# Self-attention's row products regrouped: five groups of four matmuls a step, and seven PSUM banks handed out as one set

## The chip, the cores and the metric

The kernel runs on one NeuronCore of a Trainium2 chip. Its time is the device time of one execution in microseconds (us). The kernel before took 2029.76 us (median of 3 runs, 2025.14 to 2033.86).

## The reference

Two transformer blocks act on `x` of shape (4, 1024, 256): cross attention over 64 context rows, then a self-attention block with a mixture of experts, then a second cross attention and a second mixture of experts. The change lies in the self-attention, of which this is the core (16 heads of width 16, 1024 rows a batch):

```python
scores = jnp.einsum('bhqd,bhkd->bhqk', q, k) / np.float32(np.sqrt(hd))
scale = jax.nn.sigmoid(jnp.einsum('bhsd,hd->bhs', q, scale_w)) * 2.0
scores = scores * scale[..., None]
aw = jax.nn.softmax(scores, axis=-1)
out = jnp.einsum('bhqk,bhkd->bhqd', aw, v).transpose(0, 2, 1, 3).reshape(b, s, d)
```

A softmax takes the row's maximum off before the exponential, and the kernel computes that maximum exactly.

## The kernel before

**Units and steps.** Self-attention is cut into 32 units: a batch, half of its queries (512), and four heads (L658, class `Unit`). Each unit takes eight steps in each of two passes.

- The first pass (`first`, L677) multiplies queries by keys so that a query is a PSUM partition, and VectorE takes the maximum of 512 keys at a time (L694). A step makes four such products, one for each head.
- The second pass (`second`, L712) runs LEAD = 11 steps behind. It multiplies the other way round, so that a key is a partition, adds the negated maxima with a product of ones (`ones_r`, `self.m`), and ScalarE takes the exponential out of PSUM (L726). A step makes four of these too.
- `weigh` (L728) multiplies the exponentials of the step before by the values and adds the result up in the bank `acc`.

Queries and keys are kept as a leading and a remaining half side by side, so that a product of one head has a contraction of 32 rows. Each first product is two matmuls (parts f0 and f1 below), each second product three (s0, s1 and s2, the one with ones). All are 512 columns wide. Head j of a unit sits on partitions 32j to 32j+31, so that the matmuls of the four heads use different rows of the PE array and can run side by side. I call such a set of up to four a group, heads 0 and 1 the low heads and heads 2 and 3 the high heads.

**The order of a step.** It is written out by hand in the loop at the end of `self_attention` (L623); TensorE and VectorE keep the program's order (`in_order`). `round_` (L953) is called twice, with `weigh` between the calls:

| group | before, from row groups of low heads | from row groups of high heads |
|---|---|---|
| 1 | s0 | f0 |
| 2 | s1 | f1 |
| 3 | s2 | none |
| | weigh (four column groups) | |
| 4 | f0 | s0 |
| 5 | f1 | s1 |
| 6 | none | s2 |

After group 6 come the fillers: small pieces of other work which `on(step)` doles out by a credit of 1.5 a step, among them the transposes and products that bring a later tile in (`enter`), turn the maxima (`maxima`, L697) or the accumulated result (`done`, L740), and finish a tile (`leave`). A filler takes one PSUM bank, which ScalarE or VectorE reads out. In the order of each engine the read of a filler follows the exponentials and the maxima of its step.

**PSUM.** Of eight banks one is `acc`. Three rotate for first products (pool `first`), four rotate for second products and fillers (pool `bank`). A new tile in a bank waits until the last reader of the bank's former tile is done. In the eleven steps before the second pass starts, the first products take every other tile from `bank`.

Of the kernel before, what the change touches and what calls it, by code (L numbers as in the profile page):

```python
# [26 lines left out]
ALU = mybir.AluOpType  # L27
AX = mybir.AxisListType
# [3 lines left out]
P = 128  # L32
# [36 lines left out]
def two_blocks(  # L69
# [19 lines left out]
    nc = tc.nc  # L89
# [3 lines left out]
    banks = {}  # L93

    @contextmanager
    def psum(stage, **bufs):

        with ExitStack() as stack:
            for tag, n in bufs.items():
                pool = tc.tile_pool(name=f"{stage}_{tag}", bufs=n, space=PSUM, reuse_waits="tile")  # L100
                banks[tag] = stack.enter_context(pool)
            yield

    def new(pool, shape, tag, dt=F32, bufs=None):
        return pool.tile(shape, dt, tag=tag, name=tag, bufs=bufs)

    def two_banks():
        return new(banks["two_banks"], [P, 1024], "two_banks")

    def bank():  # L110
        return new(banks["bank"], [P, 512], "bank")

    def side():
        return bank()[:, :256]
# [4 lines left out]
    def placed(engine, ins):  # L119
        return tc.keep_in_program_order(ins) if engine in in_order else ins  # L120

    def matmul(*args, **kw):
        return placed(nc.tensor, nc.tensor.matmul(*args, **kw))  # L123
# [7 lines left out]
    def on_dve(ins):  # L131
        return placed(nc.vector, ins)
# [64 lines left out]
    def on_all(pool, first, n, queue, width=D):  # L197

        at = ROWS.index(first) * D
        t = new(pool, [P, n, width], f"row_{first}")  # L200
        queue.dma_start(
            out=t.rearrange("p n d -> p (n d)"), in_=rows[at : at + n * width].partition_broadcast(P)
        )
        return [t[:, i] for i in range(n)]
# [304 lines left out]
    class Entrance:  # L509


        def __init__(self, even, pool):
            self.pool = pool
            self.k_rows = [new(even, [P, 4, S], "k_rows0", F32R)]
            self.vals_1 = [new(even, [P, TB * H * K1 + ROW], "vals_10")]
            self.wq4 = new(pool, [P, 2, D], "wq4")

            self.wz = new(pool, [P, 2, P], "wz")
            self.gb_half = new(pool, [P, 2], "gb_half")
            at = ROWS.index("gb") * D  # L520
            nc.scalar.dma_start(out=self.gb_half, in_=rows[at : at + D].rearrange("(m p) -> p m", p=P))
            self.n1g, self.n1b = on_all(pool, "n1g", 2, nc.scalar)
            (self.moe_gb,) = on_all(pool, "last", 1, nc.scalar, E)
# [99 lines left out]
    def self_attention(ent, first_batch):  # L623
# [3 lines left out]


        with tc.tile_pool(name="sa1", bufs=1) as one, tc.tile_pool(name="sa2", bufs=2) as work:
            acc = new(banks["acc"], [P, 512], "acc")  # L630
            gb_half, n1g, n1b, moe_gb = ent.gb_half, ent.n1g, ent.n1b, ent.moe_gb
            ent.k_rows.append(new(one, [P, 4, S], "k_rows1", F32R))
            ent.vals_1.append(new(one, [P, TB * H * K1 + ROW], "vals_11"))
# [24 lines left out]
            class Unit:  # L658
# [15 lines left out]
                    self.part = new(small, [P, 4, 4, 2], "tops", bufs=3)  # L674
                    yield 0

                def first(self, s, js, half, alone):  # L677

                    assert self.b["entered"] == TB
                    i, at = s // 2, s % 2  # L680
                    for j in js:
                        if half == 0:
                            self.ps[j] = bank() if alone and j % 2 else new(banks["first"], [P, 512], "first")
                        r = slice(j * ROW, (j + 1) * ROW)
                        matmul(
                            self.ps[j],
                            self.q[r, half, i * P : (i + 1) * P],
                            self.b["k"][r, self.g, at * 512 : (at + 1) * 512],
                            start=half == 0,
                            stop=half == 1,  # L690
                        )
                        if half:
                            on_dve(
                                nc.vector.tensor_reduce(self.part[:, i, j, at : at + 1], self.ps[j], AX.X, ALU.max)  # L694
                            )

                def maxima(self):  # L697
                    top = new(small, [P, 4, 4], "top4", bufs=2)
# [13 lines left out]
                def second(self, k, js, part):  # L712

                    if part == 0 and js[0] == 0:
                        self.es.append(new(work, [P, 4, 512], "e"))
                    for j in js:
                        if part == 0:
                            self.ps[j, 2] = bank()
                        ps = self.ps[j, 2]
                        r = slice(j * ROW, (j + 1) * ROW)  # L720
                        if part < 2:
                            keys = self.b["k"][r, self.g, k * P : (k + 1) * P]
                            matmul(ps, keys, self.q[r, part], start=part == 0, stop=False)
                        else:
                            matmul(ps, ones_r[r], self.m[r], start=False, stop=True)
                            nc.scalar.activation(self.es[k][:, j], ps, AF.Exp)  # L726

                def weigh(self, k):  # L728

                    for j in range(4):  # L730
                        v = (k * H + 4 * self.g + j) * K1
                        matmul(
                            acc[j * ROW : (j + 1) * ROW],
                            self.b["v_flat"][:, v : v + ROW],
                            self.es[k][:, j],
                            start=k == 0,
                            stop=k == TB - 1,
                        )
# [74 lines left out]

            first = new(one, [P, E], "first")
            nc.vector.tensor_scalar(first, iota_e, float(E), None, ALU.subtract)
            nc.vector.tensor_copy(next_row, region)
            low = new(one, [P, 4, E], "low")
# [130 lines left out]
            for step in range(-6, 8 * NU + 80):  # L948
                n1, n2 = step // 8, (step - LEAD) // 8
                k2 = (step - LEAD) % 8  # L950
                u1, u2 = units.get(n1) if step >= 0 else None, units.get(n2) if step >= LEAD else None

                def round_(js, others):  # L953
                    for part in range(3):
                        if u2:
                            u2.second(k2, js, part)
                        if u1 and part < 2:
                            u1.first(step % 8, others, part, False)

                if u1 and not u2:  # L960
                    for part in range(2):
                        u1.first(step % 8, range(4), part, True)
                else:
                    round_((0, 1), (2, 3))
                before_ = step - LEAD - 1
                if 0 <= before_ < 8 * NU:
                    units[before_ // 8].weigh(before_ % 8)
                if u2:
                    round_((2, 3), (0, 1))
                of_units.extend(make() for make in starts.pop(step, ()))  # L970
                on(step)
            in_order.clear()
# [419 lines left out]
    with tc.tile_pool(name="sa0", bufs=1) as even, tc.tile_pool(name="sae", bufs=1) as early:  # L1392
        with psum("xa", two_banks=2, bank=4), tc.tile_pool(name="xa0", bufs=1) as xa0:

            keys_0 = cross_keys(xa0, 0, xw0, nc.scalar)
            nc.scalar.dma_start(out=fw_sb, in_=fw.rearrange("(c p) n -> p c n", p=P))
            ent = Entrance(even, early)
            first_batch = ent.batch(0)
            entering = {}
            enter_steps = ("stats", 0), ("norm", 1), ("turn", 2), ("keys", 3), ("values", 3), ("queries", 3)  # L1400
            enter_steps += ("spread", 3), ("scale", 4), ("gain", 4)

            def beside(work, r):

                if r == 4:
                    ent.prepare()
                i = r - FIRST_IN
                if 0 <= i < TB:
                    entering[i] = Enter(ent, first_batch, i, i, work, True)
                for name, behind in enter_steps:  # L1410
                    if i - behind in entering:
                        getattr(entering[i - behind], name)()

            cross_attention(0, *keys_0, beside=beside)


        with psum("sa", first=3, bank=4, acc=1):
            self_attention(ent, first_batch)
    ctx.enter_context(psum("rest", two_banks=2, bank=4))
    xa1 = ctx.enter_context(tc.tile_pool(name="xa1", bufs=1, reuse_waits="tile"))  # L1420
    keys_1 = cross_keys(xa1, 1, xw1, nc.sync)
# [89 lines left out]
```

## Time and profile before

| | before |
|---|---|
| median of 3 runs | 2029.76 us |
| the profiled execution | 2037.0 us |
| its span on the chip | 2035.3 us |
| TensorE clock granted over the span | 0.945 of full speed |
| matmuls busy over the span | 1809.2 us (89%) |
| VectorE busy | 1410.0 us (69%) |
| ScalarE busy | 1054.2 us (52%) |
| weigh's first and last matmul start (L123, `acc<-e,vals`) | 305.5 and 1302.1 us |

Busy times are those of one profiled execution. In rows of the trace a group is named by engine, line, operation and what it writes and reads, with its count. A bracket at the end says how long the engine had been idle before and who released it. PE is TensorE's matmuls and PEld its weight loads. First products are `first<-k_rows,q_rows`, parts s0 and s1 are `bank<-q_rows,k_rows`, s2 is `bank<-m_rows,ones_r`. All matmuls are recorded by one helper and so have one line, L123.

### The profile page before, as it was taken

What the parts mean: (1) busy time and instruction counts of PE and PEld (TensorE: products, weight loads), DVE (VectorE), ACT (ScalarE), POOL (GpSimd) and SP (SyncE); (2) the same over time, 40 slices, a digit from 0 to 9 for tenths busy, and PEclk for the clock granted to TensorE, in tenths of its full rate; (3) what the DMA queues carried; (4) which work ended last, traced back from release to release, by engine and by line L of the source; (5) the groups of instructions that cost most, each with busy time, mean ns of one, the idle gap of its engine ahead of it and who ended that gap; (6) DMA issues with size and microseconds to landing.
All of it is one profiled execution on the core that took longest, in us unless ns stands there. A gap on an engine that the chain in (4) does not pass through costs nothing. (4 is left out here: it accounts for less than half of the span.)

```text
span 2035.3 us, 36897 instructions
## 1 busy us (share of the span) xinstructions
PE 1809.2 (89%) x13602; PEld 1078.8 (53%) x13602; DVE 1410.0 (69%) x2914; ACT 1054.2 (52%) x2202; POOL 839.8 (41%) x1260
## 2 busy tenths in 40 slices
PE   5998779999999999999999999879996888727997
PEld 4666644355454454554544444446664666524665
DVE  6998467877778777787787877267775878663221
ACT  2666416766666666666666666523333666501111
POOL 4888531022232322221322212136667888503433
PEclk7999869999999999999999999979997999958999
DMA  9998120010110101110101100068882311103542
GB/s 263 209 212 150 31 63 22 22 32 22 32 35 19 43 22 23 35 28 22 43 19 50 32 17 1 12 222 261 270 255 71 122 60 58 50 0 76 136 83 32
DMA packets 143443, 160.62 MB, mean 79 GB/s; under 512 B 24976, under 2 KB 116624, under 8 KB 143264
## 3 DMA queue, kind: packets, MB, share of 16 engines
q1 hardware_dynamic: 123552, 128.33, 25.2%
q0 software_dynamic: 9216, 16.93, 3.9%
q10 hardware_dynamic: 10496, 13.01, 1.9%
q8 instruction: 108, 1.77, 0.4%
q14 instruction: 71, 0.58, 0.1%
HBM read 77.33 MB, written 55.72 MB: 65 GB/s over the span
## 5 line engine op out<-in xcount | busy, mean ns | idle before, releaser
L694 DVE TENSOR_REDUCE tops<-first 128x1 f32<-128x512 f32 x1002 | 645.2, 685 | 213.8 <-PE first L123 191.3
L726 ACT ACTIVATE e<-bank 128x512 f32<-128x512 f32 x1024 | 555.0, 595 | 326.6 <-PE bank L123 316.1
L123 PE MATMUL first<-k_rows,q_rows 32*128 32x512 f32 x2004 | 413.8, 454 | 35.9 <-DVE tops L694 29.0
L123 PE MATMUL bank<-q_rows,k_rows 32*128 32x512 f32 x2048 | 408.2, 451 | 0.3
L123 PEld LDWEIGHTS bank<-q_rows,k_rows 32*128 32x128 f32 x2048 | 175.1, 184 | 261.7 <-issue 135.1
L123 PE MATMUL acc<-e,vals 128*32 128x512 f32 x2048 | 286.2, 612 | 0.0
L123 PE MATMUL bank<-m_rows,ones_r 32*128 32x512 f32 x1024 | 220.0, 393 | 0.0
L123 PEld LDWEIGHTS first<-k_rows,q_rows 32*128 32x128 f32 x2004 | 169.9, 186 | 73.6 <-DVE tops L694 62.2
L220 POOL TENSOR_SCALAR rstd<-mv 128x1 f32<-128x1 f32 x206 | 49.4, 240 | 331.7 <-DVE mv L219 322.4
L412 POOL TENSOR_TENSOR pr<-pr,w_sum 128x1024 f32<-128x1024 f32 x64 | 126.2, 1972 | 8.3 <-DVE w_sum L409 6.4
L221 POOL TENSOR_TENSOR rstd<-rstd,mhalf 128x1 f32<-128x1 f32 x206 | 121.5, 590 | 17.2
L420 ACT COPY pr_t<-two_banks 128x1024 f32<-128x1024 f32 x64 | 64.8, 1012 | 117.0 <-PE two_banks L126 117.0
L123 PEld LDWEIGHTS bank<-m_rows,ones_r 32*128 32x128 f32 x1024 | 112.4, 185 | 14.2
L123 PE MATMUL two_banks<-xg_t,ew 128*128 128x512 f32 (+1 forms) x288 | 112.9, 550 | 0.0
L549 POOL CAST qst<-en_th 128x256 fp32r<-128x256 f32 x32 | 13.3, 416 | 216.8 <-DVE en_th L603 216.8
L123 PEld LDWEIGHTS acc<-e,vals 128*32 128x32 f32 x2048 | 42.8, 108 | 102.2 <-issue 92.3
L126 PE MATMUL two_banks<-ident,pr 128*128 128x128 f32 x512 | 72.0, 285 | 27.7 <-POOL pr L412 27.5
L1361 ACT ACTIVATE h_t<-two_banks 128x512 f32<-128x512 f32 (+1 forms) x36 | 19.8, 549 | 144.6 <-PE two_banks L123 144.6
L254 POOL DMA_INDIRECT out_x<-y,tok_i x32 | 50.3, 1573 | 101.2 <-DMA out_x<-y,tok_i 33.5
L1362 DVE TENSOR_TENSOR h_t<-h_t,two_banks 128x512 f32<-128x512 f32 (+1 forms) x36 | 22.6, 627 | 95.7 <-ACT h_t L1361 95.7
L126 PEld LDWEIGHTS two_banks<-ident,pr 128*128 128x128 f32 x512 | 57.7, 145 | 50.0 <-POOL pr L412 49.1
L123 PE MATMUL bank<-xw,o_t 128*128 128x256 f32 x256 | 70.6, 398 | 14.2 <-ACT q_t L366 10.7
(297 smaller groups left out, 3412.1 us busy)
## 6 DMA issues: line engine op xcount, KB each, us to landing
w_s<-in_w SPq DMA_DIRECT2D x78, 512.0 KB, 5.2
xs_d<-zeros SPq DMA_DIRECT2D x8, 4112.0 KB, 52.4
q_rows<-qst SPq DMA_DIRECT2D x128, 128.0 KB, 2.4
k_rows<-kst SPq DMA_DIRECT2D x128, 64.0 KB, 2.0
ew<-in_e SPq DMA_DIRECT2D x15, 512.0 KB, 4.1
x_s<-xs_d SPq DMA_DIRECT2D x39, 128.5 KB, 4.3
ys_d<-y ACTq DMA_DIRECT2D x39, 128.0 KB, 3.5
ew<-in_e ACTq DMA_DIRECT2D x9, 512.0 KB, 6.1
```

The source lines that it names most:

```text
L123: return placed(nc.tensor, nc.tensor.matmul(*args, **kw))
L126: return placed(nc.tensor, nc.tensor.transpose(*args))
L220: on_pool(nc.gpsimd.tensor_scalar(r, mv[:, 1:2], EPS, None, ALU.add))
L221: on_pool(nc.gpsimd.tensor_tensor(r, r, mhalf, ALU.pow))
L254: return nc.gpsimd.indirect_dma_start(out=dst[:], out_offset=bass.IndirectOffsetOnAxis(ap=idx, axis=0), in_=src[:], in_offset=None, comput ...
L412: on_pool(nc.gpsimd.tensor_tensor(self.pr, self.pr, self.w.unsqueeze(2).to_broadcast(bc), ALU.mult))
L420: on_act(nc.scalar.copy(self.pr_t.rearrange("p j q -> p (j q)"), tp))
L549: on_pool(nc.gpsimd.tensor_copy(dst[:, 0], src))
L694: nc.vector.tensor_reduce(self.part[:, i, j, at : at + 1], self.ps[j], AX.X, ALU.max)
L726: nc.scalar.activation(self.es[k][:, j], ps, AF.Exp)
L1361: on_act(nc.scalar.activation(h, ps[:, :n], AF.Silu))
L1362: on_dve(nc.vector.tensor_tensor(h, h, ps[:, CAP : CAP + n], ALU.mult))
```

## The change

The third and sixth half-filled groups are merged with neighbours, so that a step has five groups of four:

| group | from row groups of low heads | from row groups of high heads |
|---|---|---|
| 1 | s0 | f0 |
| 2 | s1 | f1 |
| 3 | s2 | s0 |
| | weigh | |
| 4 | f0 | s1 |
| 5 | f1 | s2 |

The high heads' s0 now stands ahead of `weigh`. The number of matmuls is the same. The orders of VectorE, POOL and the DMA queues are the same too, and ScalarE's differs in one place of 2260.

The pools `first` and `bank` give way to seven single banks, from which a class picks while the program is written: the bank that was let go longest ago by its own count. A bank of a second product counts as let go when its exponential is recorded, one of a first product two counts later than its maximum is recorded, and a filler's at once.

```diff
+    class Banks:
+        def __init__(self, n):
+            self.count, self.let_go = 0, {f"any{i}": i - n for i in range(n)}
+        def take(self):
+            tag = min((t for t in self.let_go if self.let_go[t] is not None), key=self.let_go.get)
+            self.let_go[tag] = None
+            return tag, new(banks[tag], [P, 512], tag)
+        def give(self, tag, behind=0):
+            self.let_go[tag] = self.count + behind
+            self.count += 1
+        def brief(self):
+            tag, t = self.take()
+            self.give(tag)
+            return t
...
     def bank():
-        return new(banks["bank"], [P, 512], "bank")
+        return any_bank[-1].brief() if any_bank else new(banks["bank"], [P, 512], "bank")
...
-                            self.ps[j] = bank() if alone and j % 2 else new(banks["first"], [P, 512], "first")
+                            self.ps[j] = choice.take()
+                        tag, ps = self.ps[j]
...
+                            choice.give(tag, 2)
...
-                            self.ps[j, 2] = bank()
-                        ps = self.ps[j, 2]
+                            self.ps[j, 2] = choice.take()
+                        tag, ps = self.ps[j, 2]
...
                             nc.scalar.activation(self.es[k][:, j], ps, AF.Exp)
+                            choice.give(tag)
...
-                    round_((0, 1), (2, 3))
+                    shared((u2, lo, "s0"), (u1, hi, "f0"))
+                    shared((u2, lo, "s1"), (u1, hi, "f1"))
+                    shared((u2, lo, "s2"), (u2, hi, "s0"))
                 before_ = step - LEAD - 1
                 if 0 <= before_ < 8 * NU:
                     units[before_ // 8].weigh(before_ % 8)
                 if u2:
-                    round_((2, 3), (0, 1))
+                    shared((u2, hi, "s1"), (u1, lo, "f0"))
+                    shared((u2, hi, "s2"), (u1, lo, "f1"))
...
-        with psum("sa", first=3, bank=4, acc=1):
+        with psum("sa", **{f"any{i}": 1 for i in range(7)}, acc=1):
+            any_bank.append(Banks(7))
             self_attention(ent, first_batch)
+            any_bank.pop()
```

More of the change, by code (lines that the diff above doesn't have):

```diff
@@ L108, in two_banks @@
         return new(banks["two_banks"], [P, 1024], "two_banks")
+    class Banks:
[12 more added lines that the diff above has]
+            return t
+    any_bank = []
     def bank():
-        return new(banks["bank"], [P, 512], "bank")
+        return any_bank[-1].brief() if any_bank else new(banks["bank"], [P, 512], "bank")
     def side():
@@ L629, in self_attention @@
         with tc.tile_pool(name="sa1", bufs=1) as one, tc.tile_pool(name="sa2", bufs=2) as work:
-            acc = new(banks["acc"], [P, 512], "acc")
+            acc, choice = new(banks["acc"], [P, 512], "acc"), any_bank[-1]
             gb_half, n1g, n1b, moe_gb = ent.gb_half, ent.n1g, ent.n1b, ent.moe_gb
@@ L675, in spread, with first @@
                     yield 0
-                def first(self, s, js, half, alone):
+                def first(self, s, js, half):
                     assert self.b["entered"] == TB
@@ L682, in first @@
                         if half == 0:
-                            self.ps[j] = bank() if alone and j % 2 else new(banks["first"], [P, 512], "first")
+                            self.ps[j] = choice.take()
+                        tag, ps = self.ps[j]
                         r = slice(j * ROW, (j + 1) * ROW)
                         matmul(
-                            self.ps[j],
+                            ps,
                             self.q[r, half, i * P : (i + 1) * P],
@@ L692, in first @@
                         if half:
-                            on_dve(
-                                nc.vector.tensor_reduce(self.part[:, i, j, at : at + 1], self.ps[j], AX.X, ALU.max)
-                            )
+                            on_dve(nc.vector.tensor_reduce(self.part[:, i, j, at : at + 1], ps, AX.X, ALU.max))
+                            choice.give(tag, 2)
                 def maxima(self):
@@ L951, in self_attention, with shared @@
                 u1, u2 = units.get(n1) if step >= 0 else None, units.get(n2) if step >= LEAD else None
[L953 to L958, printed above, removed]
+                def shared(*group):
+                    for u, js, part in group:
+                        if u is None:
+                            continue
+                        if part[0] == "s":
+                            u.second(k2, js, int(part[1]))
+                        else:
+                            u.first(step % 8, js, int(part[1]))
+                lo, hi = (0, 1), (2, 3)
                 if u1 and not u2:
-                    for part in range(2):
-                        u1.first(step % 8, range(4), part, True)
-                else:
-                    round_((0, 1), (2, 3))
+                    shared((u1, range(4), "f0"))
+                    shared((u1, range(4), "f1"))
+                else:
+                    shared((u2, lo, "s0"), (u1, hi, "f0"))
+                    shared((u2, lo, "s1"), (u1, hi, "f1"))
+                    shared((u2, lo, "s2"), (u2, hi, "s0"))
                 before_ = step - LEAD - 1
```

## The prediction

> **What bounds the kernel now.** I read the stretches first. The change acts only where self-attention runs, between 300 and 1305 us. There each stretch looks like this one (columns: length, then busy us and count of PE, PEld, DVE, ACT, POOL, then the granted clock):
>
> ```profile
> core 0: us, PE busy (x) PEld busy (x) DVE busy (x) ACT busy (x) POOL busy (x), PEclk, DMA share, GB/s
> 600.00:900.00 300.00, 294.19 (x2559) 153.32 (x2556) 228.93 (x481) 193.78 (x398) 82.52 (x136) 0.98 0.12 29
> ```
>
> TensorE looks full, at 98%. But the ends of matmuls are modelled, so the waits have to be read too, those of the weight loads between 340 and 1270 us:
>
> ```profile
> PEld bank L123 <- issue: 147.6, 255, 1.7
> PEld bank L123 <- ACT e L726: 91.7, 178, 0.8
> PEld acc L123 <- issue: 85.7, 232, 0.7
> PEld first L123 <- DVE tops L694: 51.9, 72, 1.8
> ```
>
> "Issue" waits are loads that run ahead of the matmuls. The second and fourth rows are real: a product waits for a bank that an exponential or a maximum has not let go. Not all of their length stops the array, since loads lead it. So I follow one step in order of time, from one weigh (706.80) to the next (710.33):
>
> ```profile
> 706.80 1.06 PE L123 MATMUL acc<-e,vals 128*32 128x512 f32 x8
> ...
> 707.80 0.49 PE L123 MATMUL bank<-q_rows,k_rows 32*128 32x512 f32 x2
> ...
> 708.13 0.40 PE L123 MATMUL bank<-q_rows,k_rows 32*128 32x512 f32 x2
> ...
> 708.37 0.40 PE L123 MATMUL bank<-m_rows,ones_r 32*128 32x512 f32 x2
> ...
> 708.61 1.29 DVE L694 TENSOR_REDUCE tops<-first 128x1 f32<-128x512 f32 x2 [0.62 <-PE first L123]
> ...
> 708.70 0.44 PE L126 MATMUL bank<-ident,o 128*128 128x128 f32 x2
> ...
> 708.79 1.09 ACT L726 ACTIVATE e<-bank 128x512 f32<-128x512 f32 x2 [0.73 <-PE bank L123]
> ...
> 709.06 0.18 PEld L123 LDWEIGHTS bank<-q_rows,k_rows 32*128 32x128 f32 x1 [0.17 <-issue]
> ...
> 709.43 0.18 PEld L123 LDWEIGHTS bank<-q_rows,k_rows 32*128 32x128 f32 x1 [0.19 <-ACT e L726]
> ...
> 710.33 0.16 PEld L123 LDWEIGHTS acc<-e,vals 128*32 128x32 f32 x8 [0.37 <-issue]
> ```
>
> Counted from the weigh: group 4 at +1.00, group 5 at +1.33, group 6 (the high heads' s2 alone) at +1.57, a filler of two transposes at +1.90, the next step's first s0 at +2.26. The second s0 comes only at +2.63: it needs the bank of the high heads' first exponential, which started at +1.99. So a bank is free 0.64 us after its exponential starts. The next weigh follows 0.90 later: 3.53 us a step, of which 0.37 is this wait.
>
> I sorted 241 steady steps by their fillers (the program's order has the fillers, the trace's `acc` records the times, weigh to weigh). Steps without a filler (44): 37 near 3.19, held by the maximum that frees the last of three `first` banks. With one (85): 60 are bound by the exponential's bank, most at 3.53. With two (106): 4.01 to 4.97, 76 bound by TensorE, 30 by the second exponential's bank (4.02). With three (6): 4.5 to 5.8. TensorE is the limit in about 100 steps, a bank's release in the others.
>
> **The change, part by part.** *The sixth group goes.* Its price is the distance of two groups, 708.37 - 708.13 = 0.24 us, exact in any step that TensorE bounds. If all steps were so, 256 x 0.24 would give 61 us; less the steps that it can't reach, about 56.
>
> [...]
>
> *Where the stall goes: later exponentials, earlier demand.* The high heads' s2 moves from +1.57 to group 5, +1.33. Their exponentials start at +1.75 and +2.24, their banks are free at +2.39 and +2.88. Before, a one-filler step asked only the first of these banks for the next group 1. The changed program's order, read with its bank numbers, asks for both: in 85 of 85 one-filler steps the next step's high first products (f0) take exactly these two banks. The last of group 1 thus comes at +2.88. Its row of the array then has f1 (0.34 later), s0 (0.23 later), and weigh 0.32 after that: +3.77, where before it was 3.53. The trace has such a late fourth member at 1194.39 us, with part 1 of the others starting beside it and weigh 0.67 later; the added s0 in that row (0.23) makes it about 0.89.
>
> *s0 of the high heads ahead of weigh.* It needs banks 1.3 us earlier in the step, and these are often a filler's. Where VectorE reads the filler, that read stands behind both low maxima. Dearest is the transposed `acc_sb` of `done`:
>
> ```profile
> 1190.11 1.29 DVE L694 TENSOR_REDUCE tops<-first 128x1 f32<-128x512 f32 x2 [0.60 <-PE first L123]
> 1190.22 0.66 PE L126 MATMUL bank<-ident,acc_sb 128*128 128x128 f32 x4
> ...
> 1191.59 0.42 DVE L754 TENSOR_TENSOR o<-bank,sums 128x256 f32<-128x256 f32 x1
> ```
>
> The weigh was at 1188.32, the read ends at +3.69, the bank is free by +3.75, and weigh can't come before +4.07. While s0 waits, weigh and everything behind it on TensorE's queue wait too, and so do the next exponentials.
>
> The sum by kind of step:
> - No filler, 44: the fourth of group 1 takes the bank free at +2.39, so 2.39 + 0.89 = 3.28 against 3.19: 44 x 0.09 = +4.0.
> - One filler, 40 that were at 3.53: +0.24 each, +9.6. Fifteen with `acc_sb`: 4.07 - 3.54 = 0.53, +8.0. Twelve with eight matmuls in the filler: 3.86 to 3.77, -1.1. Four whose bank is read into `src`: +1.6. Fourteen others, mostly held by the maxima's own chain: 0. Together +18.1.
> - Two fillers, 106: 35 stay bound by TensorE, -6.7 (a few late maxima gain nothing). Twelve fall from 4.01 to the release, 3.78: -2.8. In 59 the second filler's bank or a late VectorE read ends the wait, from -0.2 to +0.4 each: +1.9. Together -7.5.
> - Three fillers: -0.6. The eleven last steps, second pass only, where weigh waits for the last exponential: 7 x -0.22 = -1.5.
>
> That is 4.0 + 18.1 - 7.5 - 0.6 - 1.5 = +12.5 us. The first eleven steps are bound by the maxima, 4 x 0.61, whichever banks they use: 0, between -1 and +1. Instruction counts, other engines' orders and DMAs don't change: 0, since no wait of theirs is moved past anything.
>
> *What the trace doesn't show* is f0 waiting for an exponential's bank with s0 in the same row behind it. Below, the fourth member could come with no more cost than 0.67: then 0.2 less in about 140 steps, -28, near -15 in all. Above, every stall could repeat behind late maxima or filler reads: some 0.1 in 150 steps, +15. The nearest row (1194.39) gives the middle. Seven banks as one set also make the maxima's lag harmless more often; in the trace that lag appears in few steps outside the unit boundaries, so I take 0, and 5 us as its bound.
>
> The profiled execution was 2037.0 us (span 2035.3), 7 above the median of the runs. The difference goes onto the median: 2029.8 + 12.5 = 2042.3.
>
> **The rivals.**
> - *TensorE is the bound throughout* (other side). One mechanism: group 6 is gone in every step and the banks are let go in time because the choice runs over seven. For it speaks 98% PE; against it the 709.43 wait. It gives 2029.8 - 56 = 1974 if whole. It decides as soon as the last bank asked for by group 1 is free before +2.4. With the part-way case (two late banks cost 0.67, not 0.89) about 2015. Chance 0.14.
> - *Gains and losses cancel*: the two-filler steps gain their full 0.24 (-25), one-filler steps lose as reckoned. 2029.8 + 4.0 + 18.1 - 25 = 2027, up to 2039. Chance 0.28.
> - *VectorE's reads get in the way more often*: a late maximum now holds second products as well, since banks are shared. Fifty two-filler steps lose 0.3 instead of gaining: 2029.8 + 12.5 + 15 = 2057. Chance 0.13.
> - *The groups don't fill*: s2 and s0 of different heads not side by side. Mixed groups of s and s2 start within 45 ns of each other in the trace (36 such), so I give it nothing apart.
>
> **How the numbers follow.** A measurement of this kernel can tell about 0.5% (10 us) from no change. Likeliest is the release-bound case, 2042 (0.45), its own range 2034 to 2050; with the VectorE case slower holds 0.58. Same has 0.28, faster 0.14. The range reaches down into the part-way case and up to the VectorE case: 2016 to 2058.
>
> **What would show it.** Matmuls with f0 waiting on ACT e, at the fourth member of group 1. One-filler steps at 3.77 instead of 3.53, `acc_sb` steps near 4.07, steps without a filler near 3.28, steps of two eight-matmul fillers 0.22 shorter. The stretch from 305 to 1302 us longer by about 12, everything after it the same. If one-filler steps come out at 3.3 or less, the release chain is wrong and the kernel is faster.

## The result, and the profile after

The changed kernel takes 2048.24 us (median of 5 runs, 2047.19 to 2049.81). The kernel before, run beside it five times on the same chip, takes 2029.76 (2024.16 to 2035.86). The ratio is 1.0092, with a 95% interval of 1.0065 to 1.0119: 18.5 us slower, between 13 and 24.

The stretch from weigh's first to its last start was 996.6 us long and is now 1011.5. As before, the columns are length, busy us and count of PE, PEld, DVE, ACT and POOL, then the granted clock. First the kernel before:

```profile
305.50:1302.10 996.60, 969.24 (x8452) 483.35 (x8451) 747.10 (x1550) 653.92 (x1318) 232.74 (x390) 0.99 0.11 27
```

And after, with the same 300 us in the middle of it that the prediction showed:

```profile
302.10:1313.60 1011.50, 975.37 (x8449) 473.51 (x8449) 742.55 (x1551) 656.40 (x1318) 232.89 (x390) 0.99 0.11 27
```

```profile
600.00:900.00 300.00, 292.24 (x2532) 148.03 (x2529) 225.22 (x471) 193.06 (x394) 82.90 (x136) 0.99 0.12 29
```

PE's busy time rose by 6 us with no matmul added. A matmul's end is modelled, so a busy PE holds waiting too. The count tells more: 2559 matmuls in those 300 us before, 2532 now. The waits of the weight loads (us in total, times, longest), between 340 and 1280 us:

```profile
PEld any L148 <- issue: 244.8, 388, 1.5
PEld any L148 <- ACT e L751: 77.3, 224, 0.9
PEld acc L148 <- issue: 70.3, 234, 0.7
PEld any L148 <- DVE tops L719: 24.6, 44, 2.0
```

The wait for exponentials is still there: 224 times, 178 before in the same window. First and second products and fillers are all `any` now, so one row holds the waits of all of them. Below is an `acc_sb` step (weigh at 649.37, its first half left out) and the step after it:

```profile
652.68 0.42 DVE L780 TENSOR_TENSOR o<-any,sums 128x256 f32<-128x256 f32 x1
653.25 0.47 PE L148 MATMUL any<-q_rows,k_rows 32*128 32x512 f32 x1 [0.25 <-DVE o L780]
653.64 1.07 PE L148 MATMUL acc<-e,vals 128*32 128x512 f32 x8
...
655.39 1.08 ACT L751 ACTIVATE e<-any 128x512 f32<-128x512 f32 x2 [1.19 <-PE any L148]
...
656.04 0.18 PEld L148 LDWEIGHTS any<-k_rows,q_rows 32*128 32x128 f32 x1 [0.18 <-ACT e L751]
656.53 0.18 PEld L148 LDWEIGHTS any<-k_rows,q_rows 32*128 32x128 f32 x1 [0.31 <-ACT e L751]
...
657.11 0.39 PE L148 MATMUL any<-q_rows,k_rows 32*128 32x512 f32 x1
...
657.43 0.16 PEld L148 LDWEIGHTS acc<-e,vals 128*32 128x32 f32 x8 [0.37 <-issue]
```

In the upper part a high head's s0 (653.25) waits until VectorE has read the filler (652.68 + 0.42), and weigh (653.64) stands behind it: 4.27 us for that step. Then the light case. The exponentials start at +1.75 from weigh, the two high f0 follow at +2.40 and +2.89 as their banks come free, the last s0 of that row at +3.47, and the next weigh at +3.79 (657.43).

### The profile page after: what moved, and what is told of

The parts are those of the page before. It is cut to its first block, busy times and chain, and to the rows that moved or that the text cites. A ratio compares the mean times of both kernels' runs of the same rounds, so it can differ in the third digit from the quotient of the medians.

```text
span 2046.4 us, 36897 instructions
## 1 busy us (share of the span) xinstructions
PE 1811.8 (89%) x13602; PEld 1069.7 (52%) x13602; DVE 1403.9 (69%) x2914; ACT 1057.2 (52%) x2202; POOL 840.1 (41%) x1260
## 5 line engine op out<-in xcount | busy, mean ns | idle before, releaser
L719 DVE TENSOR_REDUCE tops<-any 128x1 f32<-128x512 f32 x1024 | 653.4, 683 | 238.5 <-PE any L148 235.0
L751 ACT ACTIVATE e<-any 128x512 f32<-128x512 f32 x1024 | 555.0, 595 | 334.8 <-PE any L148 333.2
L148 PE MATMUL any<-k_rows,q_rows 32*128 32x512 f32 x2048 | 435.3, 459 | 37.2 <-ACT e L751 16.1
L148 PE MATMUL any<-q_rows,k_rows 32*128 32x512 f32 x2048 | 457.3, 463 | 7.0 <-DVE o L780 4.0
L148 PEld LDWEIGHTS any<-q_rows,k_rows 32*128 32x128 f32 x2048 | 202.9, 183 | 291.8 <-issue 226.0
L148 PEld LDWEIGHTS any<-k_rows,q_rows 32*128 32x128 f32 x2048 | 182.8, 187 | 99.6 <-ACT e L751 59.7
L148 PE MATMUL any<-m_rows,ones_r 32*128 32x512 f32 x1024 | 203.0, 393 | 0.0
L148 PEld LDWEIGHTS any<-m_rows,ones_r 32*128 32x128 f32 x1024 | 96.6, 185 | 3.1
L148 PE MATMUL bank<-xw,o_t 128*128 128x256 f32 x256 | 70.9, 400 | 13.5 <-ACT q_t L391 10.5
```

Of the source, the lines that this page charges most:

```text
L719: on_dve(nc.vector.tensor_reduce(self.part[:, i, j, at : at + 1], ps, AX.X, ALU.max))
```

## The experiments

Each kernel was run on the same chip as the kernel before, and the ratio is to that. Chips differ from group to group (e1 to e4; e5 and e6; e2 again, e8 and e9; e10 and e11), so ratios can be compared down the table and medians only within a group.

| kernel | groups | banks | median, us | before beside it | ratio (95%) |
|---|---|---|---|---|---|
| the change | 5 | seven, by count | 2048.24 | 2029.76 | 1.0092 (1.0065 to 1.0119) |
| e1 | 5 | the old pools | 2053.42 | 2026.25 | 1.0124 (1.0099 to 1.0148) |
| e2 | 6 | seven, by count | 2005.52 | 2026.25 | 0.9892 (0.9872 to 0.9912) |
| e2 again | 6 | seven, by count | 2016.43 | 2035.93 | 0.9900 (0.9879 to 0.9920) |
| e3 | 5 | by release time | 2019.72 | 2026.25 | 0.9960 (0.9939 to 0.9981) |
| e4 | 5 | count, filler later | 2111.00 | 2026.25 | 1.0417 (1.0395 to 1.0439) |
| e5 | 6 | by release time | 2023.91 | 2033.01 | 0.9957 (0.9943 to 0.9970) |
| e6 | 5 or 6 | by release time | 2011.30 | 2033.01 | 0.9894 (0.9877 to 0.9911) |
| e8 | 5 or 6 | by count | 2016.98 | 2035.93 | 0.9904 (0.9885 to 0.9923) |
| e9 | 5 or 6 | release time, maxima 0.4 later | 2002.97 | 2035.93 | 0.9837 (0.9817 to 0.9858) |
| e10 | 5 | as the change, short reads | 1975.69 | 2038.22 | 0.9702 (0.9682 to 0.9722) |
| e11 | 6 | as before, short reads | 1976.37 | 2038.22 | 0.9693 (0.9672 to 0.9714) |

The medians of the kinds of step, weigh to weigh in us, from one trace of each:

| step | before | change | e1 | e2 | e3 | e4 | e9 | e10 | e11 |
|---|---|---|---|---|---|---|---|---|---|
| no filler (44) | 3.19 | 3.33 | 3.47 | 3.30 | 3.32 | 3.33 | 3.31 | 3.09 | 2.92 |
| one: `xr` (14) | 3.53 | 3.79 | 3.59 | 3.34 | 3.60 | 3.79 | 3.31 | 3.36 | 3.32 |
| one: `acc_sb` (15) | 3.53 | 4.28 | 4.28 | 3.37 | 3.60 | 3.78 | 3.24 | 3.75 | 3.37 |
| two of eight matmuls (5) | 4.76 | 4.55 | 4.60 | 4.76 | 4.60 | 5.60 | 4.60 | 4.55 | 4.76 |
| `en_f`, then `o` (5) | 4.01 | 3.87 | 3.87 | 3.79 | 3.79 | 6.40 | 3.56 | 3.54 | 3.65 |

**Each half alone.** e1 keeps the five groups and has the old pools back:

```diff
...
-        with psum("sa", **{f"any{i}": 1 for i in range(7)}, acc=1):
+        with psum("sa", first=3, bank=4, acc=1):
...
```

> The five groups alone, with the pools of before (three banks for first products, four for second products and fillers). Theory (release-bound: group 1's last bank and the filler's bank under the high heads' s0 set the step): group 1 now waits for the first low maximum's bank (+2.52) and not for the second high exponential's (+2.88), so most one-filler steps fall from 3.79 to about 3.41; steps without a filler 3.41; acc_sb steps stay at 4.28, since the filler's bank still goes to the high heads' s0; two-filler steps as in the change. About 13 us under the change, 2035, level with before within 10. Rival (the regrouping itself costs, whatever the banks): as the change, 2048. Rival (TensorE bound): 1974.

Measured 2053.42: a miss in the direction. `acc_sb` steps are 4.28 as expected, but light steps are 3.59, not 3.41. There a high head's s0 takes the filler's bank also when the filler is a light one, and follows its read. The five groups are slower by themselves; the new choice of banks didn't bring the loss.

e2 has the seven banks and the six groups:

```diff
-                    shared((u2, lo, "s2"), (u2, hi, "s0"))
+                    shared((u2, lo, "s2"))
...
-                    shared((u2, hi, "s1"), (u1, lo, "f0"))
-                    shared((u2, hi, "s2"), (u1, lo, "f1"))
+                    shared((u2, hi, "s0"), (u1, lo, "f0"))
+                    shared((u2, hi, "s1"), (u1, lo, "f1"))
+                    shared((u2, hi, "s2"))
```

> The seven banks by choice alone, in the six groups of before. Theory: no filler's bank stands under a product ahead of weigh, and a late fourth product of group 1 costs only 0.67, so one-filler steps come at 3.3 instead of 3.53, two-filler steps at 3.8 to 3.9 where they were at 4.01, the rest as before: about -15 us against before, 2015. Rival (the shared choice of banks is what costs, in any order): 2035 or more. Rival (no bank matters): 2030.

Measured 2005.52, better than expected, and faster than the kernel before. Its light steps fall from 3.53 to about 3.3 with no group less. Here is one with the filler `xr` (weigh at 501.84):

```profile
503.82 1.09 ACT L751 ACTIVATE e<-any 128x512 f32<-128x512 f32 x2 [0.73 <-PE any L148]
504.09 0.50 PE L148 MATMUL any<-q_rows,k_rows 32*128 32x512 f32 x2
504.38 0.58 PE L148 MATMUL any<-k_rows,q_rows 32*128 32x512 f32 x2
504.47 0.50 PE L148 MATMUL any<-q_rows,k_rows 32*128 32x512 f32 x2
504.72 0.48 PE L148 MATMUL any<-k_rows,q_rows 32*128 32x512 f32 x2
504.81 0.39 PE L148 MATMUL any<-m_rows,ones_r 32*128 32x512 f32 x2
505.13 0.64 PE L148 MATMUL acc<-e,vals 128*32 128x512 f32 x4
```

The exponentials start at +1.98, so the first of their banks is free at +2.62, as in the kernel before. Before, that bank held up the second s0 of a low head: s0, s1, s2, weigh, 0.90 us. Here both s0 run at once (504.09), and the late bank goes to an f0 of a high head, the second in the row of 504.38. It starts 0.09 after the first, at 504.47: f0, f1, weigh, 0.66 us. The same release costs 0.24 less, because a high row has two parts ahead of weigh and a low row three.

e3 has five groups and picks the bank by an estimate of the time after weigh at which it comes free (the four numbers are for heads 0 to 3, 3.6 is for a filler):

```diff
-                            choice.give(tag, 2)
+                            choice.give(tag, (2.52, 3.13, 0.60, 1.20)[j])
...
-                            choice.give(tag)
+                            choice.give(tag, (0.75, 1.24, 2.39, 2.88)[j])
...
-            self.give(tag)
+            self.give(tag, 3.6)
```

> The five groups with the seven banks given out by the time after weigh at which this trace lets them go (first high maximum 0.60, low exponentials 0.75 and 1.24, second high maximum 1.20, high exponentials 2.39 and 2.88, low maxima 2.52 and 3.13, fillers 3.6), instead of by a count. Theory: group 1's last bank is free at +2.52 in one-filler steps and s0 of the high heads gets the second low maximum's, so 3.45 to 3.52 instead of 3.79, acc_sb steps no longer 4.28; two-filler steps -0.2 against before: 1995 to 2005. Rival (the regrouping itself costs): 2040 or more.

Measured 2019.72, some 15 us above the expectation and 20 below its rival. `acc_sb` steps lose their wait (4.28 to 3.60), but a light step is 3.60: a high head's s0 now waits for the bank of the second low maximum, free near +3.15, and weigh follows 0.4 later. With five groups a step asks for two banks more before weigh, one for each high head's s0, whatever the choice.

e4 is the change with a filler's bank counted four places later:

```diff
-            self.give(tag)
+            self.give(tag, 4)
```

> The change, but a filler's bank counts as let go four places later, so that s0 of the high heads never takes it in a one-filler step. Group 1 takes the same banks as in the change. Theory: acc_sb steps fall from 4.28 to 3.79, src steps from 4.39 to 3.79, other one-filler steps stay at 3.79; in two-filler steps some 8 us less: 2028 to 2034, level with before. Rival (VectorE's reads don't matter, only the exponentials' banks do): as the change, 2048.

Measured 2111.0. The steps that it was made for did as expected: `acc_sb` 4.28 to 3.78, `src` 4.39 to 3.80. But 56 steps with two fillers got over 0.3 us longer than in the change. In the one below (weigh at 573.70) s0 has the bank of a first product of its own step:

```profile
576.61 0.18 PEld L148 LDWEIGHTS any<-q_rows,k_rows 32*128 32x128 f32 x2
...
577.16 0.39 PE L148 MATMUL any<-q_rows,k_rows 32*128 32x512 f32 x1
...
578.95 1.28 DVE L719 TENSOR_REDUCE tops<-any 128x1 f32<-128x512 f32 x2
579.67 0.18 PEld L148 LDWEIGHTS any<-q_rows,k_rows 32*128 32x128 f32 x1 [2.56 <-DVE tops L719]
579.68 0.49 PE L148 MATMUL any<-q_rows,k_rows 32*128 32x512 f32 x1 [2.12 <-DVE tops L719]
580.10 0.16 PEld L148 LDWEIGHTS acc<-e,vals 128*32 128x32 f32 x8 [0.24 <-issue]
```

One s0 starts at 577.16. Its neighbour waits until VectorE, late with other work, has read the bank (the maximum at 578.95), and weigh is held with it: 6.40 us for the step. The rival that an s0 ahead of weigh puts VectorE in weigh's way is seen here at its full price.

**Both in one.** e5 is e3's choice with six groups. e6 merges groups only in steps whose fillers should be long enough to cover the exponentials, and has the timed choice. `PRODUCT` is what the kernel's planner reckons for a product (1.1 us), `FOUR` for the transposes of four tiles, as of `m_pad` or `acc_sb`:

```diff
...
+                five[0] = sum(spent) >= PRODUCT and FOUR not in spent
...
-                    shared((u2, lo, "s2"), (u2, hi, "s0"))
+                    shared((u2, lo, "s2"), *([(u2, hi, "s0")] if five[0] else []))
...
```

> The six groups of before with the seven banks given out by the time after weigh at which the trace lets them go (as in the third kernel, with 2.63 and 3.12 for the high exponentials). Theory: group 1's last bank is free at +2.52 to +2.63 in every step with up to two fillers, and no product ahead of weigh takes a filler's bank, so steps without a filler 3.19 to 3.30, with one 3.2 to 3.4 unless TensorE bounds them, the others as with the count: 1998 to 2006, at most 7 us under the seven banks by count with six groups (2005.5). Rival (the count's choice was already right for six groups): 2005.

> Five groups only in steps behind fillers of 1.1 us or more by the planner's own costs and without a transposed unit (m_pad, acc_sb); six groups in all others; banks by release time. Theory: a step gains the sixth group's 0.22 only where TensorE bounds it, and pays for the regrouping only where a release bounds it, so taking five groups in about 80 TensorE-bound steps gives -10 to -17 us against six groups throughout: 1988 to 1996. Rival (the regrouping costs wherever it is used, since s0 ahead of weigh meets fillers' banks): 2005 to 2020.

e5 took 2023.91: a miss, with a ratio of 0.9957 where e2 has 0.9892. Its steps without a filler have the same 3.19 as before, but a late VectorE costs it more: between 340 and 1280 us its weight loads wait 142.6 us for maxima, 105.1 in e2, and the four steps with `m_pad` and `fw_sb,g_t` take 4.80 us, 4.25 in e2. That this is all of it isn't shown. e6 took 2011.30, which is 12.6 less than e5 beside it and within the expected gain over six groups. Its own forecast, 1988 to 1996, was built on e5's and missed by 15.

Three more on one chip. e8 is e6's mixture with the change's count; e9 is the mixture with timed choice, and every bank that a maximum reads counted 0.4 us later (in five-group steps the high exponentials' banks too, by 0.24). Against e6:

```diff
...
-                            choice.give(tag, (2.52, 3.13, 0.60, 1.20)[j])
+                            choice.give(tag, (2.92, 3.53, 1.00, 1.60)[j])
...
```

> The six groups of before with the seven banks picked by the change's count, once more, as the yardstick for the two kernels beside it. Ratio to before near 0.989 again (0.986 to 0.992). If it comes near 0.996, the gain of the free choice of banks depends on the chip or the run, and not on which bank a product gets.

> Five groups only in steps whose fillers cost at least one product and hold no eight-matmul transposes of four tiles, six groups elsewhere; banks by the change's count. If the count is the better choice with six groups because it keeps a maximum's bank back longest, then this is 2 to 12 us faster than six groups with the count (ratio to before 0.983 to 0.988): the two-filler steps that TensorE bounds lose 0.22 us each. The rival says the count puts the high heads' first part onto the filler's bank in the five-group steps, as in the change, so that acc_sb steps are 4.28 again and nothing is gained over six groups.

> The same mixture of five and six groups, banks by release time, but every bank that VectorE's maximum reads is counted 0.4 us later than it comes free in a steady step. Then the next step's second low first product takes an exponential's bank in every step and a late maximum has 0.4 us in hand. If lateness of VectorE was what the choice by time lost against the count, this gives 1990 to 2000 us (ratio 0.981 to 0.985), steps without a filler after maxima near 3.30. If lateness isn't the cause, it stays near the mixture without the 0.4 us (ratio 0.989).

e2 repeats its ratio. e8 gains nothing over it, as its rival said: in the traces two-filler steps gain 4.0 us in sum and the others give some 2 back (`src` 4.18; `acc_sb` 3.56, and not the 4.28 that the rival named), and the medians are level. e9 is 13.5 us below e2 beside it, and 33 below the kernel before, with its ratio in the expected range: merged groups where they are covered, and banks chosen with time in hand for VectorE. What each of its two changes of the release times brought isn't shown. e9 is the fastest kernel here that computes all of it.

**Shorter reads.** e10 and e11 are the changed kernel and the one before with maxima and exponentials of 256 columns (in e10 0.42 and 0.38 us each, where the kernel before has 0.69 and 0.60 with 512). `weigh` reads these 256 twice, and the other columns are left out. In e10:

```diff
...
-                            nc.scalar.activation(self.es[k][:, j], ps, AF.Exp)
+                            nc.scalar.activation(self.es[k][:, j, :256], ps[:, :256], AF.Exp)
...
```

> The changed kernel, but each maximum and each exponential reads only the first 256 of its bank's 512 columns (weigh reads those 256 twice), so that every bank is let go about 0.25 us sooner and the chains of four take about half; the maxima and exponentials of the other columns are left out. TensorE's instructions are unchanged. If the release of banks is what ate the gain, TensorE now bounds nearly every step and this is 45 to 56 us faster than six groups with the same shortening, near 1935 to 1950 us (ratio to before near 0.957). If merging the groups costs TensorE something itself (s2 and s0 not side by side, or row groups changing more often), it gains little over six groups even here.

> The kernel before with the same shortening (first 256 columns for maxima and exponentials, the other columns left out). Its waits for a bank go: steps without a filler from 3.19 to about 2.95, one-filler steps from 3.53 to about 3.2, some 40 us in all, so near 1990 us (ratio 0.98). If the kernel before was bound by TensorE and not by the release of banks, it stays near 2030.

Both came out at 1976 us. e11 gained 62 us, more than expected. In its trace weigh starts 12.1 us earlier (293.4 for 305.5), as the eleven steps ahead of it hold first products and their maxima alone, and the stretch from weigh to weigh is 45.4 us shorter, with the same matmuls. So waits for these reads were a bound of the kernel before. e10 missed by 26 us at the near end: five groups were no faster than six, even with banks free sooner (in e10 0.43 us after an exponential's start, 332.97 to 333.40, for 0.64 before). The reason stands in a step without filler. First e11 (weigh at 333.49):

```profile
335.75 0.18 PEld L123 LDWEIGHTS first<-k_rows,q_rows 32*128 32x128 f32 x1 [0.50 <-DVE tops L694]
335.75 0.18 PEld L123 LDWEIGHTS bank<-q_rows,k_rows 32*128 32x128 f32 x2
...
336.09 0.39 PE L123 MATMUL bank<-m_rows,ones_r 32*128 32x512 f32 x2
...
336.41 0.16 PEld L123 LDWEIGHTS acc<-e,vals 128*32 128x32 f32 x8 [0.36 <-issue]
```

And e10 (weigh at 331.19):

```profile
333.40 0.50 PE L148 MATMUL any<-k_rows,q_rows 32*128 32x512 f32 x1 [0.23 <-ACT e L751]
...
333.75 0.39 PE L148 MATMUL any<-m_rows,ones_r 32*128 32x512 f32 x2
...
333.82 0.54 PE L148 MATMUL any<-q_rows,k_rows 32*128 32x512 f32 x2
...
334.29 0.16 PEld L148 LDWEIGHTS acc<-e,vals 128*32 128x32 f32 x8 [0.36 <-issue]
```

In e11 the late f0 (+2.26) is 0.66 ahead of weigh, in e10 (+2.21) it is 0.89 ahead: the s0 added to its row. So e10 comes 0.17 later although its bank was free sooner. In e10's light steps the halved reads let the last high f0 start at +2.47: with 0.89 that is 3.36, as measured. The expectation had taken the shortening to be enough to leave TensorE as the bound, and it wasn't. Where it is, in the two-filler steps, e10 is 12.2 us shorter than e11 in sum (435.4 to 447.6), about 0.12 a step.

## Why the prediction was right, and which terms were off

The mechanism held: weigh waits for the fourth member of group 1, which waits for an exponential's bank. The measured 2048.24 is 6 above the 2042 forecast and inside its range, and the sign is the likeliest one. Its closeness is in part luck: the stretch came within 2.4 us of the forecast 12.5 because terms that were 9 us too low met others that were 7 too high. Step by step:

- *The sixth group's 0.24 us.* Seen where TensorE bounds: steps of two eight-matmul fillers went from 4.76 to 4.55.
- *Exponentials at +1.75 and the fourth member at +2.88.* Measured +1.75 and +2.89 (655.39 and 656.53).
- *The late row with f1, s0 and weigh behind it: +3.77.* Light steps came out at 3.79 to 3.81. That the added s0 makes the cost 0.89 and not 0.67, which the trace of before didn't show, is what e10 and e11 show side by side.
- *No filler, 3.28, +4.0.* The median is 3.33, the sum +2.1: the common step is 0.05 longer, and a few late ones got shorter.
- *`acc_sb`, +8.0.* This is the term that was mis-sized: 4.28 and +11.1. VectorE's read ends at +3.74 (reckoned 3.69), s0 follows 0.15 later (0.06), weigh 0.40 after that (0.32): 0.21 in each of 15. All one-filler steps together: +24.1 for +18.1.
- *Two fillers, -7.5.* Measured -4.5. The steps that pair `fw_sb,g_t` with `acc_sb` or with `o` lost 0.5 and 0.47 us each, ten in all; I had allowed up to 0.4.
- *Three fillers -0.6, tail -1.5.* Measured -3.5 and -3.7 (eleven steps, 31.1 us in sum for 34.8, most at 2.88 for 3.11); three steps at the start of the stretch add 0.3.
- *The first eleven steps, 0.* The maxima start 0.60 apart there in the kernel before (267.63, 268.23, 268.82 and so on), near the 0.61 of the forecast. Measured -3.4 against the profiled execution, -0.7 against a second profile of the kernel before. That one was taken because the first lay 7 us above the median; at 2036.9 us it wasn't nearer to it.

The classes add up to +14.8, the whole stretch to +14.9, and to +12.6 against the second profile. Against that one, steps with one and with two fillers come out much the same (some +22 and -4), but those with none at -2 and those with three at 0: the sums of these two classes are no larger than the difference between two profiles of one kernel, so they say little of the change. The medians differ by 18.5. The rest, 3.6 to 5.9 us, the traces don't settle. Half-clock time could be a part of it: of the profiled stretch 20.4 us ran at half the clock before and 10.2 after, which by an estimate from these two (half of what lies between them) hides up to 5 us of the difference. But the second profile of before, with 0.95 of the clock granted over its span as in the change (0.945 in the first), differs by less.

*The rivals.* "TensorE is the bound throughout" fell: five groups with the old pools, with the count, and with short reads all wait. It was put as a matter of when banks come free, "before +2.4". The runs show a second condition that I had only inside the 0.89: which row the late bank serves. The empty half of group 3 was no idle time in a step with a late bank; it was the slack in which a high row caught up. Merging takes that slack from the high rows, in all steps, and returns 0.21 us only in steps where no row is late. "Gains and losses cancel" fell with the two-filler steps, which gained 4.5 us and not 25. VectorE in weigh's way came true in part, in the `acc_sb` and `g_t` steps. "The groups don't fill" fell: where nothing is late, s2 and s0 start 0.02 apart. In the changed kernel:

```profile
708.87 0.40 PE L148 MATMUL any<-m_rows,ones_r 32*128 32x512 f32 x2
708.89 0.41 PE L148 MATMUL any<-q_rows,k_rows 32*128 32x512 f32 x2
```

What I hadn't priced is the other half of the change. I took the seven banks as nearly nothing (0, bound 5 us). Alone (e2) they are worth some 21 us, for the most part because the count gives a late bank to a row with two parts. The change's loss is so the sum of a gain of 21 and of a regrouping that costs about 39 on top of it (18.5 + 20.7, the two differences from before). In e1, with the old pools, the regrouping costs 27: the two halves don't simply add, and under five groups the seven banks are worth about 9 (27.2 - 18.5, on two chips).

## What to carry to other kernels

A half-empty slot beside a wait isn't a cost until you have checked whether the row that is late uses it to catch up; count the parts that stand between the late release and the join, for each row (here 0.66 us with the slot and 0.89 without it, in e11 and e10). When buffers come free at different times, give the latest to the consumer with the shortest way to the join (0.66 us in e2 for 0.90 before), and put nothing ahead of the join that needs one more buffer (`acc_sb` steps went from 3.53 to 4.28 us). A 98% busy engine whose ends are modelled is no proof of a bound: shorten the reads or move the releases, and see whether the time moves (62 us in e11).

## What the hardware showed beside this

At four places a stretch, about 130 us apart, no matmul starts for 1.94 to 2.15 us at a unit's boundary while the maxima finish; 1.44 to 1.65 us of this are idle by the profile, 1.45 at most in the kernel before and 1.62 at least in the change. In the trace of the kernel before, the granted clock is 0.50 for some time after each of them: 3.4, 6.8, 3.4 and 6.8 us. In that of the change it is 0.50 or 0.51 for 3.4 us after each of the last three. In the kernel before, around the second of these:

```profile
667.30 0.50 PE L123 MATMUL first<-k_rows,q_rows 32*128 32x512 f32 x1 [1.45 <-DVE tops L694]
```

```profile
660.90:667.60 6.70, 4.79 (x43) 1.80 (x38) 6.34 (x22) 3.19 (x6) 1.94 (x3) 1.00 0.01 2
667.60:674.40 6.80, 6.80 (x40) 2.75 (x34) 3.61 (x9) 2.87 (x7) 2.86 (x8) 0.51 0.00 0
```

The clock falls from 1.00 to 0.51, and PE's 6.80 us hold 40 matmuls. In the second profile of the kernel before, the same place has the same pause (1.44 us, to 665.28) and no dip:

```profile
665.30:672.10 6.80, 6.70 (x60) 3.68 (x64) 5.61 (x15) 4.54 (x12) 3.88 (x13) 1.00 0.21 49
```

In the change, the first pause is 1.65 us idle (to 539.41), longer than any in the kernel before, and the clock is 1.00 in the 6.8 us after it. So the length of the pause alone doesn't decide. Over the whole span the granted clock was 0.945 in the first profile of the kernel before and 0.95 in the second; time at half clock may be why the kernel's runs spread over 12 us, and no run isolated that.
